# The up stage of a quantised FFN in reverse order, by half tiles, and the first parts of the down stage put ahead of a branch

## The chip, the core and the metric

The kernel runs on one NeuronCore of a Trainium2 chip. The metric is the device time of one execution in microseconds (us); the time given for a kernel is the median of its runs.

## What is computed

Two blocks with residuals on x of 2 x 2048 rows of 512. First cross-attention with layernorm, then the block that matters here:

```
x    = act_qdq(layernorm(x))                  # 16-bit: one scale for the whole tensor
up   = act_qdq(x @ lpbq_dequant(w_up).T)      # w: 4-bit, 1536 x 512
gate = act_qdq(x @ lpbq_dequant(w_gate).T)
sig  = fixed_qdq_u16(sigmoid(gate))
p    = act_qdq(gate * sig)
o    = act_qdq(p * up)
y    = x_in + o @ lpbq_dequant(w_down).T
def act_qdq(x): s = max(max(abs(x)) / 32767, 1e-12); return clip(round(x / s)) * s
```

Every `act_qdq` needs the maximum over its whole tensor before one element of it can be rounded. So nothing of p can be rounded before all of gate is there, and nothing of o before all of p and all of up are there.

## The kernel before

The 4096 rows are tokens. They are cut into NG = 8 groups of TG = 512 tokens for gate and up, and into 16 steps of TD = 256 tokens (two tiles of 128) for down. The 1536 features are NF = 12 chunks of 128, taken four at a time (NQ = 4), so there are NK = 3 tiles per group and 24 tiles `n = (t, k)` in all. Four stages follow each other:

1. **Front** (attention, layernorm, the transposed rows `hT`), up to about 176 us.
2. **Gate** (lines 507 to 552). The rounded input of a group is split into exact parts (`split_integers`, line 215: a high part, a low part and a combination), 3 MB per group, which go to the matmuls and are also written out (`parts_d`, line 536). `project` (line 496) makes 8 matmuls into a PSUM tile `q` and 4 into `e` for each feature chunk, 12 in all. The results go to `gate_d` (line 551). In the idle time the weights of up and down are prepared (`steps`) and written to `wu_d` and `wd_d`.
3. **Up** (lines 554 to 628). For each group t = 0 to 7 the parts are read back (`load_group`, line 560), and for each tile the gate is read back (`load_gate`, line 565). ScalarE makes `gi`, `sig` and `sq` of it (`gelu_like`, line 579), VectorE makes the integers `pi` of p (line 610). The matmuls make u two chunks at a time; ScalarE takes q out of PSUM (line 617) and VectorE subtracts e (line 618). PSUM holds two such halves (`ps_m`, bufs=2). u and pi are written out whole, 1 MB and 0.5 MB per tile (lines 619 and 611). Each tile gives the column n of `umax` (the maximum of u, line 620) and of `pumax` (a bound of the product, `max(abs(u) * pi)`, lines 621 to 623).
4. **Down** (lines 631 to 777). The scale of o needs the maximum of the rounded product. The kernel takes, in each partition, the tile with the largest bound: `best`, `where` and `row` (lines 653 to 658) name it, two indirect DMAs of GpSimd fetch it (lines 662 and 669), it is rounded and multiplied (lines 677 to 682), and the maximum over partitions is made by GpSimd (line 686). If the second largest bound cannot exceed that maximum, and two conditions on p hold, `flag` is 1 (line 698). All engines read the flag (line 701) and branch (line 702): with 0 a long general path is run, with 1 it is jumped over. Behind the branch the scales of o are made (lines 736 to 745). Then, for each of 16 steps, the next step's p, u and x are read (`load_step`, line 641: 3 + 3 + 1 DMAs), u is rounded (`ui`, line 752), and each of two tiles of 128 tokens gives `oi` (line 756), its parts (line 759), 24 matmuls into q, 12 into e (lines 764 and 768), and the output (lines 772 to 777).

The frame that records the kernel (tile pools, a scheduler) decides the order of instructions on each engine and puts in the waits; an engine runs its instructions in that order. Two things of the built order matter below. The DMAs of SyncE (the queue SP) use eight semaphores in turn, and each waits until the one before it on its semaphore has landed: at most eight are in flight. And where the general path is jumped over, each engine first waits until all that it issued ahead of the branch is done, and then adds to its semaphores what the general path would have added, so that later waits hold for both ways. A wait of another engine for work behind the branch thus waits for that engine to have passed the branch.

Of the kernel before, what the change touches and what calls it, by code (L numbers as in the profile page):

```python
# [61 lines left out]
P = 128  # L63
# [12 lines left out]
def tile_xattn_ffn(  # L76
# [41 lines left out]
    up_d = dram.tile([NG * NK, P, NQ, TG], F32, name="up_d")  # L118
    p_d = dram.tile([NG * NK, P, NQ, TG], I16, name="p_d")
# [8 lines left out]
    umax = const.tile([P, NG * NK], F32, name="umax")  # L128
    gtop = const.tile([P, NG * NF], F32, name="gtop")
    pumax = const.tile([P, NG * NK], F32, name="pumax")  # L130
# [99 lines left out]

    with ExitStack() as c0:
# [252 lines left out]
        wp_late = ctx.enter_context(tc.tile_pool(name="wp_late", bufs=NF - NE))  # L484
        hi_pool = c0.enter_context(tc.tile_pool(name="hi", bufs=1))
# [21 lines left out]
        with ExitStack() as c2:  # L507
# [6 lines left out]
            homes = [c2.enter_context(tc.tile_pool(name="parts0", bufs=1))]  # L514
# [9 lines left out]
            homes.append(c2.enter_context(tc.tile_pool(name="parts1", bufs=1)))  # L524
# [5 lines left out]
            steps = chain(split_rows(wpp, ps_t, w_up, wu_d, "u"), split_down(wpp, ps_t))  # L530
            for t in range(NG):
# [4 lines left out]
                nc.sync.dma_start(out=parts_d[t], in_=parts.bitcast(F32))  # L536
                for k in range(NK):
# [13 lines left out]
                    nc.sync.dma_start(out=gate_d[n], in_=g4)  # L551
            advance(steps, 1000)

    with ExitStack() as c3:
        pp = c3.enter_context(tc.tile_pool(name="parts", bufs=2))
# [4 lines left out]
        def load_group(t):  # L560
            parts = pp.tile([P, 3, ND, TG], F32R, tag="parts", name=f"parts_u{t}")
            nc.sync.dma_start(out=parts.bitcast(F32), in_=parts_d[t])
            return parts

        def load_gate(n):
            gt = wk2.tile([P, NQ, TG], F32, tag="gt", name=f"gt_{n}")
            nc.sync.dma_start(out=gt, in_=gate_d[n])
            return gt

        groups = {0: load_group(0)}  # L570
        wu = [load_parts(wu_d, f, "wu") for f in range(NF)]
        gts = {0: load_gate(0)}
# [25 lines left out]
        wd = []  # L598
        for t in range(NG):
            parts = groups.pop(t)  # L600
            if t + 1 < NG:
                groups[t + 1] = load_group(t + 1)
            for k in range(NK):
                n = t * NK + k
                if n + 1 < NG * NK:
                    gts[n + 1] = load_gate(n + 1)
                u4 = wk2.tile([P, NQ, TG], F32, tag="u4", name=f"u4_{n}")
                gi, sq = gelu_like(wk2, wk1, gts.pop(n), [NQ, TG], n)
                pi = wk2.tile([P, NQ, TG], I16, tag="pi", name=f"pi_{n}")
                nc.vector.scalar_tensor_tensor(pi, gi, k_p, sq, ALU.mult, ALU.mult)  # L610
                nc.sync.dma_start(out=p_d[n], in_=pi)
                for i in range(0, NQ, 2):
                    q = ps_m.tile([P, 2, TG], F32, tag="q", name=f"q_u{n}_{i}")
                    e = ps_m.tile([P, 2, TG], F32, tag="e", name=f"e_u{n}_{i}")
                    for j in range(2):
                        project(wu[NQ * k + i + j], parts, q[:, j, :], e[:, j, :])
                    nc.scalar.activation(u4[:, i : i + 2, :], q, AF.Copy, scale=1.0 + 1.0 / BASE)  # L617
                    nc.vector.tensor_tensor(u4[:, i : i + 2, :], u4[:, i : i + 2, :], e, ALU.subtract)  # L618
                nc.sync.dma_start(out=up_d[n], in_=u4)
                abs_max(umax[:, n : n + 1], u4, AX.XY)  # L620
                ua = wk2.tile([P, NQ, TG], F32, tag="ua", name=f"ua_{n}")
                nc.scalar.activation(ua, u4, AF.Abs)
                nc.vector.tensor_tensor_reduce(ua, ua, pi, 1.0, 0.0, ALU.mult, ALU.max, pumax[:, n : n + 1])
                if t == NG - 1:
                    for f in range(NQ * k, NQ * (k + 1)):
                        w = chunk_tile([P, 3, D], "wd", f)
                        nc.sync.dma_start(out=w.bitcast(F32), in_=wd_d[f])
                        wd.append(w)


    with ExitStack() as c5:
        wk1 = c5.enter_context(tc.tile_pool(name="wkd1", bufs=1))
        wk2 = c5.enter_context(tc.tile_pool(name="wkd2", bufs=2))
        ps_y = c5.enter_context(tc.tile_pool(name="ps_y", bufs=4, space=PSUM))

        def load_p(t, v):
            g, i = divmod(t * TD, TG)
            for k in range(NK):
                nc.sync.dma_start(out=v[:, ts(k, NQ), :], in_=p_d[g * NK + k, :, :, ds(i, TD)])  # L639

        def load_step(t):
            g, i = divmod(t * TD, TG)
            pi = wk2.tile([P, NF, TD], I16, tag="p5", name=f"p5_{t}")
            load_p(t, pi)
            uv = wk2.tile([P, NF, TD], F32, tag="u5", name=f"u5_{t}")
            for k in range(NK):
                nc.sync.dma_start(out=uv[:, ts(k, NQ), :], in_=up_d[g * NK + k, :, :, ds(i, TD)])  # L647
            x1 = wk2.tile([P, TD // P, D], F32, tag="x1", name=f"x1_{t}")
            nc.sync.dma_start(out=x1, in_=x1_d[g, :, ds(i // P, TD // P), :])
            return pi, uv, x1  # L650


        best = const.tile([P, 8], F32, name="best")
        nc.vector.max(best, pumax)
        where = const.tile([P, 8], U32, name="where")
        nc.vector.max_index(where, best, pumax)
        row = const.tile([P, 1], U32, name="row")
        nc.vector.scalar_tensor_tensor(row, where[:, 0:1], float(P), lane, ALU.mult, ALU.add)
        a_u, = over_partitions(umax, name="u")
        with tc.tile_pool(name="best", bufs=1) as bp:  # L660
            ub = bp.tile([P, NQ * TG], F32, name="ub")
            nc.gpsimd.indirect_dma_start(
                out=ub,
                out_offset=None,
                in_=up_d.rearrange("n p i t -> (n p) (i t)"),
                in_offset=bass.IndirectOffsetOnAxis(ap=row, axis=0),
            )
            pb = bp.tile([P, NQ * TG], I16, name="pb")
            nc.gpsimd.indirect_dma_start(
                out=pb,  # L670
                out_offset=None,
                in_=p_d.rearrange("n p i t -> (n p) (i t)"),
                in_offset=bass.IndirectOffsetOnAxis(ap=row, axis=0),
            )
            s_u, r_u = act_scale(a_u, "u", unit)
            ui = bp.tile([P, NQ * TG], I16, name="ui_b")
            nc.scalar.activation(ui, ub, AF.Copy, scale=r_u)

            nc.vector.tensor_tensor(ub, pb, ui, ALU.mult)

            two = const.tile([P, 2], F32, name="two")
            nc.vector.tensor_reduce(two[:, 0:1], ub, AX.X, ALU.max, apply_absolute_value=True)
            nc.vector.tensor_scalar(two[:, 1:2], best[:, 1:2], r_u, 1.0 + 2.0**-18, ALU.mult, ALU.mult)
            nc.vector.tensor_scalar(two[:, 1:2], two[:, 1:2], 0.5 * (QMAX + 2.0), None, ALU.add)
        top = const.tile([P, 2], F32, name="top")
        nc.gpsimd.partition_all_reduce(top, two, P, bass_isa.ReduceOp.max)
        a_o = const.tile([P, 1], F32, name="a_o")
        nc.vector.tensor_copy(a_o, top[:, 0:1])

        neg = const.tile([P, 1], F32, name="neg")  # L690
        nc.vector.tensor_scalar(neg, r_p, NEG_P, 1.0, ALU.mult, ALU.add)
        nc.vector.tensor_scalar(neg, neg, QMAX, top[:, 1:2], ALU.mult, ALU.max)
        sure = const.tile([P, 1], F32, name="sure")
        nc.vector.tensor_tensor(sure, neg, a_o, ALU.is_le)
        ok_p = const.tile([P, 1], F32, name="ok_p")
        nc.vector.tensor_scalar(ok_p, p_top, MIN_P, None, ALU.is_ge)
        flag = const.tile([P, 1], I32, name="flag")
        nc.vector.tensor_tensor(flag, sure, ok_p, ALU.mult)

        loaded = {0: load_step(0)}  # L700
        known = nc.values_load(flag[0:1, 0:1], min_val=0, max_val=1)  # L701
        with tc.If(known == 0):
            with tc.tile_pool(name="gen", bufs=1) as gp:
                pmax = gp.tile([P, NG * NF], F32, name="pmax")
                omax = gp.tile([P, NG * NF], F32, name="omax")

                def load(m, src, name):
                    v = gp.tile([P, TG], F32, tag="v", name=f"v{name}_{m}")
                    nc.sync.dma_start(out=v, in_=src[m // NQ, :, m % NQ, :])
                    return v  # L710
# [90 lines left out]
```

## Time and profile before

| | |
|---|---|
| median of 3 runs | 1046.68 us (1046.64 to 1049.0) |
| the profiled execution | 1046.88 us, of which the span is 1045.1 us, at a mean granted TensorE clock of 0.956 |
| TensorE (PE) busy | 944.2 us, 90% of the span |
| VectorE (DVE) / ScalarE (ACT) / GpSimd (POOL) busy | 796.2 / 541.9 / 75.2 us |
| DMA | 281.83 MB, 270 GB/s over the span |
| chain that ended last | 25% PE, all of it in the down stage |

How to read it: times count from the span's start. A row of the timeline has start, duration, engine, line, operation, output<-inputs, count, and in brackets how long the engine was idle before it and what ended that. "PEld" is the weight load, "SPq" the queue of DMAs that SyncE issues; an engine name with a q is its sequencer. Slices of view 2 are 26 us each.

### The profile page before, as it was taken

How to read it: one execution, taken by the hardware profiler on the slowest of the kernel's cores; microseconds unless marked ns; L12 is line 12 of the kernel's file. 1: busy time of each engine (PE TensorE's matmuls, PEld its weight loads, DVE VectorE, ACT ScalarE, POOL GpSimd, SP SyncE). 2: the span in 40 equal slices, each digit the busy share in tenths (PEclk: the TensorE clock that was granted, in tenths of full speed). 3: DMA queues.
4: the chain of work that ended last, by engine and by line, in shares of the span. 5: the costliest groups of instructions: out<-in, count | busy, mean ns of one | idle time of the engine just before them, and what ended most of it. 6: DMA issues, size and time to landing. Idle time of an engine off the chain costs nothing. (4 is left out here: it accounts for less than half of the span.)

```text
span 1045.1 us, 11428 instructions
## 1 busy us (share of the span) xinstructions
PE 944.2 (90%) x4320; PEld 764.4 (73%) x4320; DVE 796.2 (76%) x909; ACT 541.9 (52%) x582; POOL 75.2 (7%) x66
## 2 busy tenths in 40 slices
PE   6997975999999999996999999998029999999998
PEld 6765643888888878875878888887028888888886
DVE  4588857899989988445877789779269778887782
ACT  2278786333323332236798888987234444344431
POOL 0101110000000000000000000000001221112211
PEclk9999986999999999998999999999559999999999
DMA  9196546877985887897988898889989676766520
GB/s 332 31 350 254 212 172 257 330 278 296 357 322 201 317 315 299 316 389 285 387 298 336 315 379 321 322 317 358 354 261 293 202 230 193 231 195 198 173 80 31
DMA packets 118110, 281.83 MB, mean 270 GB/s; under 512 B 5408, under 2 KB 72992, under 8 KB 105632
## 3 DMA queue, kind: packets, MB, share of 16 engines
q1 hardware_dynamic: 117232, 278.42, 73.0%
q0 software_dynamic: 288, 1.57, 0.4%
q10 hardware_dynamic: 528, 1.05, 0.3%
q8 instruction: 34, 0.56, 0.2%
q14 instruction: 28, 0.23, 0.1%
HBM read 147.85 MB, written 133.17 MB: 269 GB/s over the span
## 5 line engine op out<-in xcount | busy, mean ns | idle before, releaser
L764 PE MATMUL yq<-wd,parts_o 128*128 128x512 f32 x768 | 182.0, 393 | 48.6 <-DMA u<-up_d 48.6
L764 PEld LDWEIGHTS yq<-wd,parts_o 128*128 128x128 f32 x768 | 145.8, 190 | 79.8 <-ACT parts_o L222 49.0
L501 PE MATMUL q_u<-parts_u,wu 128*128 128x512 f32 x768 | 192.4, 393 | 9.8 <-ACT u L617 8.5
L501 PE MATMUL q_g<-parts_g,wg 128*128 128x512 f32 x768 | 194.3, 394 | 5.2 <-ACT parts_g L222 5.2
L501 PEld LDWEIGHTS q_u<-parts_u,wu 128*128 128x128 f32 x768 | 144.7, 189 | 42.7 <-ACT u L617 11.4
L501 PEld LDWEIGHTS q_g<-parts_g,wg 128*128 128x128 f32 x768 | 144.6, 189 | 36.3 <-issue 5.6
L545 ACT ACTIVATE g<-q_g 128x512 f32<-128x512 f32 x96 | 57.3, 599 | 180.3 <-PE q_g L501 175.9
L505 PE MATMUL e_g<-parts_g,wg 128*128 128x512 f32 x384 | 105.2, 393 | 0.0
L505 PE MATMUL e_u<-parts_u,wu 128*128 128x512 f32 x384 | 103.1, 390 | 0.3 <-DVE u L618 0.3
L546 DVE CUSTOM_DVE_ANT_0 g<-g,e_g 128x512 f32<-128x512 f32 x96 | 64.5, 679 | 37.3 <-PE e_g L505 36.7
L768 PE MATMUL ye<-wd,parts_o 128*128 128x512 f32 x384 | 92.2, 389 | 0.0
L610 DVE SCALAR_TENSOR_TENSOR pi<-gi,k_p,sq 128x2048 int16<-128x2048 int16 x24 | 56.3, 2347 | 45.8 <-ACT sq L586 45.8
L505 PEld LDWEIGHTS e_u<-parts_u,wu 128*128 128x128 f32 x384 | 72.4, 189 | 15.8 <-DVE u L618 0.7
L768 PEld LDWEIGHTS ye<-wd,parts_o 128*128 128x128 f32 x384 | 72.1, 188 | 15.0
L505 PEld LDWEIGHTS e_g<-parts_g,wg 128*128 128x128 f32 x384 | 72.2, 189 | 14.8
L772 ACT ACTIVATE yqs<-yq,q_o 128x512 f32<-128x512 f32 x32 | 22.1, 689 | 117.1 <-PE yq L764 117.1
L618 DVE TENSOR_TENSOR u<-u,e_u 128x1024 f32<-128x1024 f32 x48 | 58.4, 1217 | 13.7 <-ACT u L617 13.5
L774 POOL TENSOR_TENSOR qx<-yqs,x 128x512 f32<-128x512 f32 x32 | 50.1, 1567 | 226.0 <-ACT yqs L772 226.0
L222 ACT CAST parts_o<-sa_o 128x1536 fp32r<-128x1536 int16 x32 | 47.1, 1474 | 35.8 <-PE ye L768 31.6
L776 DVE SCALAR_TENSOR_TENSOR y<-ye,e_o,qx 128x512 f32<-128x512 f32 x32 | 24.0, 751 | 54.0 <-PE ye L768 44.4
L617 ACT ACTIVATE u<-q_u 128x1024 f32<-128x1024 f32 x48 | 48.1, 1017 | 30.9 <-PE q_u L501 27.9
L756 DVE SCALAR_TENSOR_TENSOR oi<-p,k_o,ui 128x1536 int16<-128x1536 int16 x32 | 58.0, 1819 | 4.5 <-ACT ui L752 2.6
(165 smaller groups left out, 1280.0 us busy)
## 6 DMA issues: line engine op xcount, KB each, us to landing
parts_d<-parts_g SPq DMA_DIRECT2D x8, 3072.0 KB, 11.1
gate_d<-g SPq DMA_DIRECT2D x24, 1024.0 KB, 5.1
parts_u<-parts_d SPq DMA_DIRECT2D x8, 3072.0 KB, 13.5
gt<-gate_d SPq DMA_DIRECT2D x24, 1024.0 KB, 10.6
up_d<-u SPq DMA_DIRECT2D x24, 1024.0 KB, 7.0
u<-up_d SPq DMA_DIRECT2D x48, 512.0 KB, 6.8
p_d<-pi SPq DMA_DIRECT2D x24, 512.0 KB, 4.3
p<-p_d SPq DMA_DIRECT2D x48, 256.0 KB, 3.8
```

What stands on the lines that cost most here:

```text
L222: nc.scalar.copy(parts[:, 0, c], a[:, c])
L501: nc.tensor.matmul(q, lhsT=w[:, s, c, :], rhs=parts[:, s, c, :], start=(c + s == 0), stop=(c + s == ND))
L505: nc.tensor.matmul(e, lhsT=w[:, 2, c, :], rhs=parts[:, 2, c, :], start=(c == 0), stop=(c == ND - 1))
L545: nc.scalar.activation(g4[:, i, :], q, AF.Copy, scale=1.0 + 1.0 / BASE)
L546: nc.vector.tensor_tensor_reduce(g4[:, i, :], g4[:, i, :], e, 1.0, LOWEST, ALU.subtract, ALU.max, gtop[:, m : m + 1])
L610: nc.vector.scalar_tensor_tensor(pi, gi, k_p, sq, ALU.mult, ALU.mult)
L617: nc.scalar.activation(u4[:, i : i + 2, :], q, AF.Copy, scale=1.0 + 1.0 / BASE)
L618: nc.vector.tensor_tensor(u4[:, i : i + 2, :], u4[:, i : i + 2, :], e, ALU.subtract)
L756: nc.vector.scalar_tensor_tensor(oi, pi[:, :, ts(j, P)], k_o, ui[:, :, ts(j, P)], ALU.mult, ALU.mult)
L764: nc.tensor.matmul(q, lhsT=parts[:, s, f, :], rhs=wd[f][:, s, :], start=(f + s == 0), stop=(f + s == NF))
L768: nc.tensor.matmul(e, lhsT=parts[:, 2, f, :], rhs=wd[f][:, 2, :], start=(f == 0), stop=(f == NF - 1))
L774: nc.gpsimd.tensor_tensor(qx, qs, x1[:, j, :], ALU.add)
```

## The change

- **Order.** The up stage runs over the groups from 7 down to 0. The parts of groups 6 and 7 stay in SBUF, in two homes of 24 KB per partition each, and are not written to `parts_d`; the weights of up are loaded inside the last gate group. The tiles of p and up are numbered by `j`, in the new order, and the down stage takes the groups in it too. The first two gate tiles are read on GpSimd's queue.
- **Half tiles.** `up_d`, `p_d` and the columns of `pumax` are by halves of a tile (two chunks): 48 of each. u is written by halves; p is still written by one DMA per tile; the step's reads become 6 + 6 + 1 DMAs. ScalarE's absolute value and VectorE's bound are made per half (`bound`).
- **Gelu ahead.** `next_gelu` makes gi, sig and sq one tile ahead of its use.
- **Last half.** The last half of u (c = 47) has no column in `pumax`; it stays in SBUF as `u_last`, and its products are made there exactly. `best` is taken over the other 47 halves as soon as the 47th bound is there, and the fetch is half as large.
- **Maximum of u.** GpSimd's reduction over partitions is replaced by a transpose on TensorE (`rows_u`) and a reduction by VectorE.
- **Branch.** The reads of the first down step are issued in the last group of up (t = 0); the scales of o and the parts of the first tile (in three pieces) stand ahead of the branch.

```diff
-                nc.sync.dma_start(out=parts_d[t], in_=parts.bitcast(F32))
+                if t < NG - 2:
+                    nc.sync.dma_start(out=parts_d[t], in_=parts.bitcast(F32))
+                else:
+                    groups[t] = parts
...
+                    if t == NG - 1:
+                        wu += [load_parts(wu_d, f, "wu") for f in range(NQ * k, NQ * (k + 1))]
...
+        gts = [load_gate(*at, nc.gpsimd) for at in order[:2]]
...
+        def bound(c, u, pi):
+            ua = wk2.tile([P, 2, TG], F32, tag="ua", name=f"ua_{c}")
+            nc.scalar.activation(ua, u, AF.Abs)
+            nc.vector.tensor_tensor_reduce(ua, ua, pi, 1.0, 0.0, ALU.mult, ALU.max, pumax[:, c : c + 1])
+            return ua
...
+        for j, (t, k) in enumerate(order):
+            if k == 0:
+                parts = groups.pop(t)
+                if t + 1 < NG and t > 0:
+                    groups[t - 1] = load_group(t - 1)
+                if t == 0:
+                    home1.__exit__(None, None, None)
+                    lds.append(ctx.enter_context(tc.tile_pool(name="ld0", bufs=1, side="right")))
+                    load_step(0)
+            u4 = wk2.tile([P, NQ, TG], F32, tag="u4", name=f"u4_{j}")
+            if j:
+                pi = integers_of_p(j)
+            for h in range(2):
+                c = 2 * j + h
+                both = slice(2 * h, 2 * h + 2)
...
+                if c + 1 < NH:
+                    nc.scalar.activation(u4[:, both, :], q, AF.Copy, scale=1.0 + 1.0 / BASE)
+                    nc.vector.tensor_tensor(u4[:, both, :], u4[:, both, :], e, ALU.subtract)
+                else:
+                    for i in range(2):
+                        v = u_last[:, i, :]
+                        nc.scalar.activation(v, q[:, i, :], AF.Copy, scale=1.0 + 1.0 / BASE)
+                        nc.vector.tensor_tensor(v, v, e[:, i, :], ALU.subtract)
+                        abs_max(umax[:, LAST + 1 + i : LAST + 2 + i], v)
+                nc.sync.dma_start(out=up_d[c], in_=u4[:, both, :] if c + 1 < NH else u_last)
+                if h == 0:
+                    next_gelu()
...
+                elif c + 2 == NH:
+                    with tc.high_priority():
+
+                        u_last = bound(c, u4[:, both, :], pi[:, both, :])
+                        ub, pb = fetch_best()
...
+        rows = ps_m.tile([P, 2, TG], F32, tag="q", name="rows_u")[:, 0, :P]
+        nc.tensor.transpose(rows, m_u.to_broadcast([P, P]), ident)
...
+        for i, (uv, pv) in enumerate([last, (ub, pb)]):
+            ui = wk2.tile([P, NQ, TG], I16, tag="gi", name=f"ui_b{i}").rearrange("p i t -> p (i t)")[:, : 2 * TG]
+            nc.scalar.activation(ui, uv, AF.Abs, scale=r_u)
+            nc.vector.tensor_tensor_reduce(uv, ui, pv, 1.0, 0.0, ALU.mult, ALU.max, two[:, i : i + 1])
...
+        def round_o(tiles, pi, ui, pieces=1):
+
+            oi, a, parts = tiles
+            cs = [ts(i, NF // pieces) for i in range(pieces)]
+            for c in cs:
+                nc.vector.scalar_tensor_tensor(oi[:, c], pi[:, c], k_o, ui[:, c], ALU.mult, ALU.mult)
+                nc.vector.tensor_scalar(a[:, c], oi[:, c], 1.0 / BASE, None, ALU.mult)
+                nc.scalar.copy(parts[:, 0, c], a[:, c])
+                nc.vector.scalar_tensor_tensor(parts[:, 1, c], a[:, c], -BASE, oi[:, c], ALU.mult, ALU.add)
+            for c in cs:
+                nc.vector.scalar_tensor_tensor(parts[:, 2, c], a[:, c], BASE + 1.0, oi[:, c], ALU.mult, ALU.subtract)
+            return parts
...
+        ui_first = up_tile(0)
+        round_up(ui_first[:, :, :P], loaded[0][1][:, :, :P])
...
+        scales_of_o(a_o)
+
+        first = o_tiles(0)
+        round_o(first, loaded[0][0][:, :, :P], ui_first[:, :, :P], 3)
+
         known = nc.values_load(flag[0:1, 0:1], min_val=0, max_val=1)
```

## The prediction

> **What bounds the kernel now.** I read the page first (PE busy 90%), then the table by stages, because an average of 90% says nothing about where the other 10% are. Columns are busy us of PE, weight load, DVE, ACT and POOL, then granted clock, DMA share and GB/s. The rows are the start of the up stage, its rest, the passage to down, and down:
>
> ```profile
> 452.78:494.68 41.90, 32.94 (x145) 26.95 (x145) 21.29 (x27) 22.72 (x18) 0.37 (x1) 0.93 0.85 330
> 494.68:728.32 233.64, 232.57 (x1008) 190.12 (x1008) 194.36 (x129) 199.61 (x127) 0.00 (x0) 0.99 0.89 337
> 728.32:776.92 48.60, 0.00 (x1) 0.00 (x0) 21.40 (x34) 14.25 (x9) 2.96 (x4) 0.53 0.85 305
> 776.92:1041.00 264.08, 264.00 (x1152) 217.84 (x1152) 203.94 (x155) 107.94 (x78) 50.15 (x32) 0.99 0.60 188
> ```
>
> In the second and fourth stretch PE is busy nearly throughout: matmuls set the time. In the third it does nothing for 48.6 us. The waits of PE between 450 and 780 us name the idle places:
>
> ```profile
> PE yq L764 <- DMA u<-up_d: 48.6, 1, 48.6
> PE q_u L501 <- ACT u L617: 8.5, 2, 8.1
> PE q_u L501 <- DVE gtop L546: 0.9, 1, 0.9
> ```
>
> The releaser named for the 48.6 us is only the event that came last by the profile; what the time consists of is seen in the timeline:
>
> ```profile
> 729.77 1.91 ACT L622 ACTIVATE ua<-u 128x2048 f32<-128x2048 f32 x1 [1.29 <-DVE u L618]
> 731.58 1.99 ACT L582 ACTIVATE gi<-gt,r_g 128x2048 int16<-128x2048 f32 x1
> ...
> 737.58 2.35 DVE L610 SCALAR_TENSOR_TENSOR pi<-gi,k_p,sq 128x2048 int16<-128x2048 int16 x1 [3.96 <-ACT sq L586]
> ...
> 742.81 0.16 DVE L658 SCALAR_TENSOR_TENSOR row<-where,lane 128x1 uint32<-128x1 uint32 x1
> ...
> 747.45 1.29 POOL L662 DMA_INDIRECT ub<-up_d,row  x1 [14.72 <-issue]
> 749.04 0.94 POOL L669 DMA_INDIRECT pb<-p_d,row  x1 [0.30 <-issue]
> ...
> 757.05 2.00 ACT L677 ACTIVATE ui_b<-ub,r_u 128x2048 int16<-128x2048 f32 x1 [19.50 <-DMA ub<-up_d,row]
> ...
> 764.69 0.16 DVE L698 TENSOR_TENSOR flag<-sure,ok_p 128x1 int32<-128x1 f32 x1
> 768.37 2.85 ACT L752 ACTIVATE ui<-u,r_u 128x3072 int16<-128x3072 f32 x1 [9.32 <-ACTq L702]
> ```
>
> From the last matmul of up (E = 728.32) the passage falls into four legs: to the row's number 14.65 (end 742.97; the gelu of the last tile is still to be made), to the fetch 4.48 (u and p must have landed), the fetch 9.60, rounding and reducing to the flag 7.80 (end 764.85), and from the flag to the first matmul 12.07. The sum is 48.6. The last leg holds the branch, which the rows of line 702 show:
>
> ```profile
> L702 DVEq COMPARE_BRANCH x1: 72/72/72, 765.5 to 765.5; - x1
> L702 DVEq EVENT_SEMAPHORE x1: 21/21/21, 768.7 to 768.7; - x1
> ```
>
> Between a sequencer's compare and its next instruction 2.7 (ACT) to 3.2 us (DVE) pass; from the flag DVE works again after 3.91 us, ACT after 3.52.
>
> **Up stage.** Ideal is 1152 matmuls at 2.72 us per 12 (the chain's rows), 261.1 us; from 452.78 to 728.32 it took 275.5. The 14.4 lost are the 0.9 and 8.1 above, 2.1 for a slow clock after the 8.1 (8 matmuls 3.78 instead of 1.98, 4 in 1.39 instead of 1.07), and 3.3 in small pieces. The 8.1 come from order: the first gate tile arrives only for 479.01, behind the weights and 3 MB of parts on SP, so p is late, and u's write waits behind p's on SP, so the third u finds no buffer.
>
> With the change, parts, weights and two gate tiles are on chip at the end of gate. GpSimd's reduction a_g stands behind its two gate reads, but these wait only for tiles 21 and 22 of gate, made 22 and 11 us before its end; I cost that at nothing (cover gone: 1 to 2 us). I walk the built order with the rows' durations, from the end of gate: r_g is there at 4.8 as before, ACT's first eviction at 7.0 to 8.0 (459.80 in the trace), then two gi, a sigmoid, an absolute value and sq (2.0 + 2.0 + 2.0 + 1.0 + 1.9 = 8.9), then the second eviction, done at 17.9. PE wants that PSUM half at 0.9 + 3 x 5.44 = 17.2: 0.7 late. VectorE then makes pi (2.35) ahead of the subtractions, and the next e tiles come 0.4, 0.7 and 0.6 late before it catches up. Sum 2.4. Later nothing should wait: per tile of 10.88 us of PE, ACT has 2 x 1.02 + 2.0 + 2.0 + 1.9 + 2 x 1.02 = 10.0 (before 9.85), DVE 2 x 1.22 + 2.35 + 2.29 + 2 x 1.2 = 9.5 (before 9.4). Slack is thin, so I charge 1.1 more. New length 0.9 + 261.1 + 3.5 = 265.5: **10.0 us gained**, bounds 4 and 12. The omitted 2 x 3 MB of parts writes and reads gain nothing by themselves: DMA ran at 337 GB/s here without ending a wait of PE, and what remains (89 MB in 265 us, 335 GB/s) asks for no more.
>
> **The passage, leg by leg, from the new E.** (1) p is ready early, so the row waits for half 46: PE is done with it at -5.44, but in the built order DVE still has pi, a bound and a maximum in front; the walk gives the subtraction at -0.8, the half maximum 1.2, the bound 1.2, and 0.7 for best and row as in the trace: row at +3.6 (0 to 4.5). (2) Half 46 must land. It leaves at +0.5, behind four weight loads of wd (3.1 MB, from about -6) and p. At the 0.41 MB/us of the busy slices here that is drained at about +4; 1.2 us of GpSimd's start as before (u landed about 746.2, issue 747.45): fetch at +6.7 (3 to 8). (3) The fetch took 9.6 for 1 MB beside full DMA engines; half a MB less at about half their rate is 2.5 less: u at +13.7, p, issued 1.6 later, at +15.3 (11 to 18). (4) Rounding is beside p's landing; bound 1.2, reduction over partitions and its hand-over 0.5, then 0.5: flag at +17.5. u_last, the transpose and the scale are done by about +12 under the fetch; without that cover they would cost up to 4. No row shows such a transpose; the 128-row matmul cannot be below zero, and 1 us above stays under cover.
>
> (5) Here the change promises most and, I think, gives nothing. The parts now stand ahead of the branch, but on DVE and ACT that means ahead of their own reading of the flag. In the built order PE's second matmul waits for a count of DVE that only the skipped-path instruction behind DVE's branch reaches. So from the flag: scales 0.9; three pieces, each 0.75 for oi, 0.25, 0.68 and 0.68 (thirds of 1.82, 0.56, 1.75 and 1.75 with some fixed cost), 7.0; then the flag and branch, 3.9. That is 11.8 against 12.07. First matmuls at +29.3. **48.6 - 29.3 = 19.3 us gained**, bounds 15 and 27.
>
> **Down.** PE has 32 x 8.16 = 261.1 us and was never short. The second tile's oi waits for DVE's branch and for SP's, which now lets five reads of u land first: about flag + 12 both, parts at flag + 16, wanted at flag + 23. The second step's p is issued behind that, parts at flag + 27, wanted at flag + 31. No loss (bounds 0 and 3). The clock: in the Trainium skill, "TensorE: Matmul & The Clock Gate", Part 1, a cold array runs at half rate until about 3.4 us of sustained work, 1.7 us lost. The rows here: the first 24 matmuls take 8.32 instead of 5.44, 2.9 lost. A gap of 29 us is still cold, so either price is paid before and after, and I count no gain.
>
> Against half tiles speaks "DMA: Bandwidth & Descriptors", section Bandwidth: batch to 1 MiB, fixed 2 us per transfer. By its fit (2 us + bytes/436 GB/s) a down step now has 15 DMAs worth 38 us in a row, more than its 16.3. But before it was 9 worth 26, also more, and PE did not wait: transfers overlap. The nearest row, 512 KB of u landing in 6.8 us, with eight in flight gives 15 x 6.8 / 8 = 12.8 us per step, under 16.3. I take the row: nothing.
>
> **Sum.** Against the profiled execution: 1046.88 - 10.0 - 19.3 = 1017.6; it lies 0.2 above the median, so **1017.4 us**.
>
> **Rivals.**
> (A) Chance 0.60: as worked out, 1009 to 1026 with its bounds.
> (B) 0.14: parts ahead of the branch do hide. PE's start would then be flag + 4.5, 7.3 less: 1010. The work order speaks for it, the wait on DVE's count against.
> (C) 0.18: ACT, at 10.0 of 10.88, never pays back its start and is in DVE's way at the end; the up stage keeps the old loss and u's half lands late: 10 less gained, 1027.
> (D) 0.06, slower: DMA count in down. Each step's 15 DMAs at eight in flight take longer than PE when one needs over 16.3 x 8 / 15 = 8.7 us. The largest before was 8.2, of twice the size. To eat 29 us over 16 steps it must be 9.7; at 10.5 us a step lasts 19.7, 16 x 3.4 = 54 lost: 1072. Half sizes and a DMA share of 0.60 speak against it.
> (E) 0.02: the sum of such mishaps leaves about 1046; that the long general path is taken would show as far above all of these.
>
> 0.3% (3.1 us) is what a measurement of this kernel can tell from no change. Faster 0.92, within 0.02, slower 0.06. The range, 1008 to 1028, holds A, most of B, and C.
>
> **What would show it.** Right: up stage of about 265 us with waits of PE under 1 us each; the fetch at E + 7; the flag at E + 17; and between flag and first matmuls still 11 to 12 us, with DVE's compare at the end of its parts. B is right if that is under 6. C if PE waits for ACT all through up. D if SP waits for DMAs in down and PE has gaps. Wrong altogether if u's last halves land over 10 us after E.

## The result, and the profile after

| | before | after |
|---|---|---|
| median of the runs compared (us) | 1047.56 (4 runs, 1046.64 to 1049.0) | 1033.94 (4 runs, 1030.94 to 1036.44) |
| ratio, 95% interval | | 0.9868 (0.9838 to 0.9897) |
| the profiled execution, its span | 1046.88, 1045.1 | 1033.99, 1032.2 |
| gate: length | 277.1 | 280.1 |
| up, from the end of gate to the last matmul | 275.5 | 269.2 |
| passage, no matmul of a stage | 48.6 | 35.2 |
| down, to its last matmul | 263.8 | 266.0 |

The change makes the kernel 1.3% faster. I had forecast 1017.4 with a range from 1008 to 1028: the direction is right, the size is not, and the time lies outside the range. Here are the stages of the kernel after, as the table by stages gives them (us, then busy us of PE, weight load, DVE, ACT and POOL, granted clock, DMA share, GB/s). The first row is gate, which I had not listed for before because I expected nothing of it:

```profile
177.33:457.40 280.07, 280.01 (x1248) 227.71 (x1248) 234.63 (x312) 88.13 (x132) 1.40 (x2) 0.99 0.77 287
457.40:726.59 269.19, 265.99 (x1153) 216.35 (x1152) 220.32 (x204) 227.24 (x170) 0.37 (x1) 1.00 0.87 327
726.59:761.78 35.19, 0.61 (x2) 0.18 (x2) 16.79 (x44) 9.12 (x10) 3.45 (x3) 0.54 0.75 296
761.78:1027.81 266.03, 264.26 (x1152) 217.72 (x1152) 205.14 (x155) 107.86 (x78) 52.94 (x32) 0.99 0.60 189
```

The end of up, E, is put here at 726.59, and in the variants at the same place. The record of the last matmul ends 0.16 us later, at 726.75, and that end is what the 275.5 and 48.6 of before and the forecast count from. By it up is 269.4 and the passage 35.0; no reading below hangs on the difference.

PE is busy throughout gate and almost throughout up, and both are still longer than 1152 matmuls at before's rate: that is a loss no list of waits can show. The waits that there are, of PE between 440 and 1030 us (total, times, longest):

```profile
PE yq L877 <- ACTq L821: 28.8, 1, 28.8
...
PE q_u L507 <- ACT u L708: 2.3, 1, 2.3
PE yq L877 <- ACT parts_o L788: 1.3, 1, 1.3
PE q_u L507 <- DVE gtop L556: 0.9, 1, 0.9
PE yq L877 <- DVE parts_o L789: 0.5, 1, 0.5
```

The 8.1 of before is a 2.3 now, as the walk of the built order had it (2.4). The long wait is still the passage, in the timeline:

```profile
726.94 0.32 SPq L716 DMA_DIRECT2D up_d<-u  x1
...
729.54 0.16 DVE L673 SCALAR_TENSOR_TENSOR row<-where,lane 128x1 uint32<-128x1 uint32 x1
...
740.51 2.10 POOL L678 DMA_INDIRECT best<-up_d,row  x1 [279.22 <-DMA wd<-wd_d]
...
749.43 1.15 ACT L752 ACTIVATE ui_b<-best,r_u 128x1024 int16<-128x1024 f32 x1 [11.15 <-DMA best<-up_d,row]
...
752.55 0.22 DVE L814 SCALAR_TENSOR_TENSOR flag<-top,floor,a_o 128x1 int32<-128x1 f32 x1
...
761.78 2.50 PE L877 MATMUL yq<-wd,parts_o 128*128 128x512 f32 x5 [28.83 <-ACTq L821]
```

From the last matmul of up (E = 726.59) the row is ready at +3.1, but GpSimd starts the fetch only at +13.9; u lands at +22.8, the flag is done at +26.2, PE starts at +35.2. Half 46 is the first row shown: it left at +0.4, and the list of DMAs gives its time from issue to landing:

```profile
up_d<-u SPq DMA_DIRECT2D x1, 512.0 KB, 12.5
```

So it landed at about +12.8, and GpSimd's start took another 1.1. (The profile names a weight load of wd as the releaser. But GpSimd waits for several semaphores here, which writes and loads use in turn, and the last weight load issued ahead of half 46, at 723.5, took 13.0 and so had landed by 736.5.)

The second loss is in the rate. A stretch of PE in gate of the kernel before, where all groups run alike, and two stretches of up in the kernel after, first one of group 5, whose parts lie in the second home, then one of group 4, in the first:

```profile
301.46 1.98 PE L501 MATMUL q_g<-parts_g,wg 128*128 128x512 f32 x8
303.27 1.07 PE L505 MATMUL e_g<-parts_g,wg 128*128 128x512 f32 x4
304.18 1.98 PE L501 MATMUL q_g<-parts_g,wg 128*128 128x512 f32 x8
...
541.46 2.04 PE L507 MATMUL q_u<-parts_u,wu 128*128 128x512 f32 x8
543.33 1.10 PE L511 MATMUL e_u<-parts_u,wu 128*128 128x512 f32 x4
544.27 2.03 PE L507 MATMUL q_u<-parts_u,wu 128*128 128x512 f32 x8
...
574.76 1.98 PE L507 MATMUL q_u<-parts_u,wu 128*128 128x512 f32 x8
576.58 1.07 PE L511 MATMUL e_u<-parts_u,wu 128*128 128x512 f32 x4
577.48 1.98 PE L507 MATMUL q_u<-parts_u,wu 128*128 128x512 f32 x8
```

From one group of eight to the next it is 2.72 us before (304.18 - 301.46), 2.81 (544.27 - 541.46) in the second home of after and 2.72 (577.48 - 574.76) in its first, without a wait in between and, in both stretches of after, at a granted clock of 1.00. All odd groups of gate and up are like the one in the second home, all even ones like the other; before, all were 2.72. An odd group is 12 x 12 matmuls and takes 33.73 us, an even one 32.67: eight passes of odd groups, four in each stage, cost some 8.5 us.

The difference to the forecast, 16.4 us of the profiled execution, is then complete: 1.6 of a later start of gate (gate starts anywhere from 175.5 to 178.4 in the runs below, and from 175.7 to 177.4 with before and its shifted variants, so no cause was sought), 3.0 in gate, 3.7 in up, 5.9 in the passage and 2.2 in down.

### The profile page after: what moved, and what is told of

Same layout as the page of the kernel before. It is cut to its first block, busy times and chain, and to the rows that moved or that the text cites. A ratio compares the mean times of both kernels' runs of the same rounds, so it can differ in the third digit from the quotient of the medians.

```text
span 1032.2 us, 11748 instructions
## 1 busy us (share of the span) xinstructions
PE 950.3 (92%) x4321; PEld 764.7 (74%) x4321; DVE 798.0 (77%) x968; ACT 541.8 (52%) x610; POOL 79.9 (8%) x67
## 5 line engine op out<-in xcount | busy, mean ns | idle before, releaser
L507 PE MATMUL q_g<-parts_g,wg 128*128 128x512 f32 x768 | 197.0, 397 | 5.0 <-ACT parts_g L225 5.0
L507 PE MATMUL q_u<-parts_u,wu 128*128 128x512 f32 x576 | 144.5, 393 | 0.0
L507 PEld LDWEIGHTS q_u<-parts_u,wu 128*128 128x128 f32 x576 | 108.3, 188 | 24.5
L511 PE MATMUL e_u<-parts_u,wu 128*128 128x512 f32 x288 | 78.1, 393 | 0.0
L662 DVE CUSTOM_DVE_ANT_0 ua<-ua,pi 128x1024 f32<-128x1024 f32 x47 | 56.9, 1221 | 18.8 <-ACT ua L661 18.8
L788 ACT CAST parts_o<-sa_o 128x1536 fp32r<-128x1536 int16 (+1 forms) x34 | 47.4, 1398 | 45.1 <-PE ye L881 27.6
L887 POOL TENSOR_TENSOR qx<-yqs,x 128x512 f32<-128x512 f32 x32 | 52.9, 1654 | 222.1 <-ACT yqs L885 222.1
L786 DVE SCALAR_TENSOR_TENSOR oi<-p,k_o,ui 128x1536 int16<-128x1536 int16 (+1 forms) x34 | 59.5, 1754 | 10.0 <-ACT ui L772 4.3
L511 PEld LDWEIGHTS e_u<-parts_u,wu 128*128 128x128 f32 x288 | 54.1, 188 | 12.2
```

The lines of the kernel that those rows point to most:

```text
L507: nc.tensor.matmul(q, lhsT=w[:, s, c, :], rhs=parts[:, s, c, :], start=(c + s == 0), stop=(c + s == ND))
L511: nc.tensor.matmul(e, lhsT=w[:, 2, c, :], rhs=parts[:, 2, c, :], start=(c == 0), stop=(c == ND - 1))
L786: nc.vector.scalar_tensor_tensor(oi[:, c], pi[:, c], k_o, ui[:, c], ALU.mult, ALU.mult)
L788: nc.scalar.copy(parts[:, 0, c], a[:, c])
L887: nc.gpsimd.tensor_tensor(qx, qs, x1[:, j, :], ALU.add)
```

## The experiments

Two theories. **Q**: the fetch is late because half 46 waits behind queued transfers, and the eight weight loads of wd in the last tiles are what fills the queue; its rival is that the row, GpSimd or the fetch itself is slow. **H**: the odd groups are slow because of where the second home lies, its address or its place; its rivals are that anything else of the new order (the transfers beside it, the kept parts) slows them. Two smaller questions are whether the parts ahead of the branch hide anything, and whether SyncE's reads ahead of it do harm. Single executions of one kernel lie up to 5.5 us apart (after: 1030.94 to 1036.44), so where a run was made once its stages are compared, not its time.

### The address of the home

In the built programs the second home of after begins at byte 204768 of each partition, 32 beyond a multiple of 64; the first at 92992, a multiple of 64. **The kernel after with the second home moved down by 32 bytes:**

```diff
+            pad1 = tc.tile_pool(name="pad1", bufs=1, side="right")
+            nc.gpsimd.memset(pad1.__enter__().tile([P, 8], F32, name="pad1"), 0.0)
             home1 = tc.tile_pool(name="parts1", bufs=1, side="right")
```

> The changed kernel with a pad of 32 bytes per partition ahead of the second home of the parts, which so begins at a multiple of 64 bytes (204736 instead of 204768). Theory: with the home 32 bytes off, 12 matmuls of an odd group take 2.81 us instead of 2.72, one part in 32 more, so that 8 odd group passes (4 in gate, 4 in up) cost 12 x 0.09 = 1.1 us each; expected 8.6 us less than the changed kernel (about 1025.3), all blocks at 2.72. Rival: it is the place at the far end of SBUF, or traffic beside it, not the 32 bytes: no difference (1033.9), odd groups still at 2.81.

Measured: ratio 0.9854 (0.9831 to 0.9877) to before; odd groups 2.79 to 2.80 per 12 matmuls, even ones 2.72. A multiple of 64 alone takes away only an eighth to a quarter of the loss.

**The kernel before, its two gate homes moved up by 32 bytes** (the same pad ahead of `parts0`):

> The kernel before with 32 bytes put ahead of its two homes of the gate stage, so that both begin 32 bytes off a multiple of 64; the up stage's buffers stay where they were. Theory of the 32 bytes: all 96 blocks of 12 matmuls in gate go from 2.72 to 2.81 us, gate longer by 8.6 us and no other stage (1047.6 to about 1056). Rival (place or traffic): no difference.

Measured: ratio 1.0064 (1.0047 to 1.0081), gate 283.0 instead of 277.1, all its groups 2.80, up untouched at 2.72:

```profile
300.52 2.03 PE L501 MATMUL q_g<-parts_g,wg 128*128 128x512 f32 x8
302.38 1.09 PE L505 MATMUL e_g<-parts_g,wg 128*128 128x512 f32 x4
303.32 2.03 PE L501 MATMUL q_g<-parts_g,wg 128*128 128x512 f32 x8
```

Only addresses (and a pad that is written once) were changed, in a kernel with the old order: 32 bytes can cost 3% of the rate of the matmuls and 2% of the stage, and the new order as a cause is not needed. In this kernel the tiles stacked above the homes (gate results, weights in preparation) moved by 32 bytes with them; in the variants of after below, the built programs differ from after in the second home and the pad alone.

**Other pads**, of 96, 1312 and 4128 bytes in the kernel after, and of 64 in the kernel before:

> The kernel after the change with the second home of the parts moved down by 96 bytes, to byte 204672 of each partition (a multiple of 128, 0x780 within 2 KB); nothing else changes. Every matmul of gate and up reads 2 KB of these parts per partition, so its start within 2 KB is that of the home. In after the odd groups, which read this home, take 2.811 us per 12 matmuls, the even ones 2.72. Theory L (the low bits of the address decide, and 128 is the unit): a multiple of 128 is at least as good as 64 beyond one, odd groups at 2.72, gate 4 us and up 4 us shorter, time 1026. Theory M (the place near the top of the memory decides): odd groups stay at 2.79 to 2.81, time 1033 to 1034. Theory N (the distance to the next 2 KB boundary decides): also slow, 2.79, and told from M by the next run.

> The same with the second home moved down by 1312 bytes, to 203456, whose low eleven bits (0x2C0) are those of the homes of the kernel before, where every group took 2.72 us per 12 matmuls. The place in the memory is nearly that of after. Theory L or N (low bits, of whatever kind): odd groups fall to 2.72, gate to 276 and up to 265, time 1026. Theory M (the place): odd groups stay at 2.79 to 2.81 and the time at 1033 to 1034.

> The kernel before the change with its two gate homes moved up by 64 bytes (to 129792 and 154368, multiples of 128, 0x300 within 2 KB); the move by 32 bytes slowed all gate groups from 2.72 to 2.80 us per 12 matmuls. Theory: a start that is a multiple of 64 is fast at this place, so 2.72 and a time of 1047. Rival: 64 beyond a multiple of 128 is what is wanted (as in all fast homes so far: 0x2C0 and 0x340), so 2.80 and 1054.

> The kernel after the change with the second home moved down by 4128 bytes, to 200640, which is 64 beyond a multiple of 128 like all homes of the kernel before (2.72 us per 12 matmuls at 92864 to 154304), and like 204736 and 203456 (2.79 to 2.80). If the place in the upper part of the memory decides, odd groups stay at 2.79 to 2.80 and the time at 1031 to 1033. If only what lies within the last 4 KB does, 2.72 and 1025.

Measured (one run each), with the two kernels above, in us per 12 matmuls; the second column is what is left of the address when it is divided by 128:

| home at byte | within 128 | us per 12 |
|---|---|---|
| 92864, 117440 (up, before), 92992, 129728, 154304 | 64 | 2.72 |
| 129792, 154368 (before, +64) | 0 | 2.75; the first group 2.80 |
| 204672 (after, 96 down) | 0 | 2.75 |
| 129760, 154336 (before, +32) | 32 | 2.80 |
| 200640, 203456, 204736 (after, 4128, 1312 and 32 down) | 64 | 2.79 to 2.80 |
| 204768 (after) | 96 | 2.81 |

With the pad of 96, a stretch of group 3 reads so:

```profile
600.92 1.99 PE L507 MATMUL q_u<-parts_u,wu 128*128 128x512 f32 x8
602.75 1.08 PE L511 MATMUL e_u<-parts_u,wu 128*128 128x512 f32 x4
603.67 1.99 PE L507 MATMUL q_u<-parts_u,wu 128*128 128x512 f32 x8
```

That is 2.75, and this run's gate is 277.8 and its up 265.6, 2.2 and 3.6 less than after: up is as long as I had forecast, with 1.3 of the slow rate left and a shorter wait (1.6). Its time was 1030.06. Only the home was moved here, so it is shown that its place changes the rate of the odd groups. Theory L of the expectation fell in its strict form (128 is better than 32 or 96, but not as good as before), and the run at 203456, with the low eleven bits of before's homes, fell too: 2.80. A theory of the place alone fails as well, since 204672 and 204736 lie 64 bytes apart. What holds in all six rows: starts that are 32 beyond a multiple of 64 are slow everywhere, and 64 beyond a multiple of 128 is the best start below byte 155000 and a bad one above byte 200000. Multiples of 128 give 2.75 in both halves of the memory, but not always. In the kernel before with 64 bytes, group 0 of gate ran at 2.80 and group 2 at 2.75, with both in the home at 129792:

```profile
201.25 2.03 PE L501 MATMUL q_g<-parts_g,wg 128*128 128x512 f32 x8
203.12 1.10 PE L505 MATMUL e_g<-parts_g,wg 128*128 128x512 f32 x4
204.05 2.03 PE L501 MATMUL q_g<-parts_g,wg 128*128 128x512 f32 x8
...
260.66 1.99 PE L501 MATMUL q_g<-parts_g,wg 128*128 128x512 f32 x8
262.49 1.08 PE L505 MATMUL e_g<-parts_g,wg 128*128 128x512 f32 x4
263.41 1.99 PE L501 MATMUL q_g<-parts_g,wg 128*128 128x512 f32 x8
```

So the address matters, but it does not fix the rate by itself. What else does, and why a start 64 beyond a multiple of 128 differs by place, stays open.

### The queue ahead of the fetch

**The eight loads left out**, to see the passage without them:

```diff
                 for f in range(NQ * k, NQ * (k + 1)):
+                    if k:
+                        wd.append(wd[f % NQ])
+                        continue
                     w = chunk_tile([P, 3, D], "wd", f)
```

> Leaves out the loads of the down weights 4 to 11; the down matmuls use chunks 0 to 3 three times, as many as before. It measures the passage with no weight traffic. Theory (queued bytes): half 46 lands within 4 us of its issue, fetch at about E + 5, and it takes 4 to 5 us instead of 8.9, so the flag stands at E + 13 instead of E + 26, first down matmul at E + 22 instead of E + 35. Rival (slow writes, slow indirect fetch): fetch not before E + 12, and 8 to 9 us long.

Measured: 1018.69 (one run), with half 46 landing 5.5 us after its issue, and this timeline (E = 723.71):

```profile
730.22 1.07 POOL L678 DMA_INDIRECT best<-up_d,row  x1 [269.74 <-DVE m_u L744]
...
735.31 1.13 ACT L755 ACTIVATE ui_b<-best,r_u 128x1024 int16<-128x1024 f32 x1
...
738.41 0.22 DVE L817 SCALAR_TENSOR_TENSOR flag<-top,floor,a_o 128x1 int32<-128x1 f32 x1
...
748.71 3.78 PE L880 MATMUL yq<-wd,parts_o 128*128 128x512 f32 x8 [18.63 <-ACTq L824]
```

The fetch starts at +6.5 (forecast: 6.7), ScalarE takes its u up 5.1 later instead of 8.9 (it landed after 4.3, when ScalarE was still busy), the flag is at +14.9, PE starts at +25.0; down takes 263.8. Passage and down together are 288.8 us instead of 301.2. So the row, GpSimd and the engines' legs are as forecast or better, and 12.4 us of the kernel after are the price of 6.3 MB that must pass just here. Theory Q holds, its rival falls.

**The loads behind the last half of u**, all eight:

```diff
-            if t == 0:
-                for f in range(NQ * k, NQ * (k + 1)):
+            if t == 0 and k != 1:
+                for f in range(NQ) if k == 0 else range(NQ, NF):
```

> The changed kernel with the loads of the down weights 4 to 7 moved behind the last write of u, to those of 8 to 11. Theory: the write of half 46 lands 12.5 us after its issue because 3 MB of weights and what stands before them are drained first; without them it lands by 6 us, GpSimd's fetch starts at about E + 7 instead of E + 13.9, and the first down matmul comes 5 to 7 us earlier (about 1028), unless the fetch, then beside 6 MB of weights, gets longer by the same. Rival: writes of u are slow by themselves: fetch still at E + 12 or later, time 1034.

Measured: ratio 0.9814 (0.9798 to 0.9831), median 1028.04. The passage (E = 724.39), half 46 landing in 5.1 us:

```profile
730.47 1.07 POOL L678 DMA_INDIRECT best<-up_d,row  x1 [270.32 <-DVE m_u L741]
...
739.42 1.15 ACT L752 ACTIVATE ui_b<-best,r_u 128x1024 int16<-128x1024 f32 x1 [3.35 <-DMA best<-up_d,row]
...
743.20 0.22 DVE L814 SCALAR_TENSOR_TENSOR flag<-top,floor,a_o 128x1 int32<-128x1 f32 x1
...
751.75 4.56 PE L877 MATMUL yq<-wd,parts_o 128*128 128x512 f32 x9 [21.01 <-ACTq L821]
```

The fetch starts at +6.1, so the 7.8 us of the loss that came ahead of it are gone. Of the rest, 2.4 in the passage and 5.8 in down against the run without the loads stay: u needs 9.0 us instead of 5.1, because the loads now run beside the fetch, and in down PE waits once 3.3 us for parts: in the built order of this kernel all reads of the second step come behind the branch, its p lands late, and VectorE's `oi` waits 3.9 us for it. Passage plus down 296.9.

**The loads behind the fetch, or behind the maximum.** Two tries to get the rest. In the first the loads stand on GpSimd's queue after the two fetches; in the second they are held until GpSimd's reduction, by a write of one element that they overwrite. Both with a moved home (203456 and 204672).

```diff
+            nc.gpsimd.tensor_copy(w[:, 0, 0:1], top[:, 0:1])
+            nc.gpsimd.dma_start(out=w.bitcast(F32), in_=wd_d[f])
```

> The kernel after the change with its eight last weight loads of down (6.3 MB) put on GpSimd's queue behind the two fetches, and the second home at 203456 as in the run before. Theory (what delayed the fetch was the drain of the loads queued ahead of half 46, and where all eight were put behind the last half they met the fetch itself): the fetch starts 6.5 us after the last matmul of up as without these loads, takes 8 us, the flag is at +15.5, first matmul at +25.5. The loads then need 6.3 MB at 0.41 MB/us, 15 us from +9, all there at +25 to +27, before PE wants the fifth chunk at +28: no wait in down. Gap 25.5 instead of 35.2: 9.7 less than after by the passage, 1024; and 8 less, 1016, if the home's address is the cause of the slow odd groups. Rival (the loads still take the fetch's share of the DMA engines, or GpSimd's eight issues hold up its reduction of the maximum): fetch to flag 12 us or more, the gap 28 to 30, PE waits for weights at down's start: 1020 to 1028.

> The kernel after the change with its eight last weight loads of down on GpSimd's queue, held there until its reduction of the two maxima is done (one element of each weight buffer is written from the result first, and the load overwrites it), and the second home of the parts at 204672 (a multiple of 128). Theory (the drain of queued loads delays the fetch, and nothing else on the path needs them early): fetch starts 6.5 us after the last matmul of up, reduction at +14, flag at +15, first matmul at +25, as without the loads. The loads are issued from +15 to +21; 6.3 MB at 0.41 MB/us are there at +31, the fifth chunk at about +19. Down as after, 264 to 266. Against after's 1033.9: passage 10 less, the slow groups 5.5 less: 1018, 1015 to 1021. Rival (PE or the other engines wait for these loads behind the branch, or the first steps' reads of p and u queue behind them): PE waits 5 us or more in down, 1023 to 1026.

Measured: 1034.34, ratio 0.9857 (0.9841 to 0.9874), and 1034.16, ratio 0.9873 (0.9857 to 0.9890). Both missed. In the first of them the built order put GpSimd's loads ahead of its fetch after all (705.8 to 724.8, one whenever a buffer of the up weights came free); with two queues feeding the DMA engines, half 46 was behind still more:

```profile
up_d<-u SPq DMA_DIRECT2D x1, 512.0 KB, 19.4
```

The fetch started at E + 21.4, PE at +41.6. It is not the test that was meant, but it is one more point on Q: more loads ahead of half 46, a later fetch. In the second the passage came out nearly as expected (fetch +6.8, flag +15.0, PE +26.2), and the cost appeared in down, 278.2 us:

```profile
PE yq L885 <- DMA wd<-wd_d: 5.0, 4, 1.6
PE yq L885 <- ACT parts_o L796: 3.9, 1, 3.9
```

PE starts and finds the last weights missing, chunk after chunk, with the granted clock at 0.71 in its first 16 us (after: 0.84). In both, as in the run without the loads, the built order also put twelve reads of u (the second and third step, 3.1 MB) ahead of the branch, where after has five; they compete with the loads, and the second step's p comes behind them. The run without the loads shows that these reads do no harm by themselves; what share of the 12 us in down is theirs and what the loads' these runs do not separate.

### The branch and its parts

**The parts of the first tile behind the branch** (`round_o` of the first tile moved into the loop, whole):

> The changed kernel with the first tile's parts made behind the branch again, as a whole and not in pieces; the scales stay ahead of it. From the flag to the first down matmul the changed kernel takes 9.0 us, the kernel before 12.1. Theory of the prediction (the branch still stands behind the parts on DVE and ACT, so putting them ahead saves little): 3.5 us of branch, then 1.8 + 0.6 + 1.5, so 7.5 to 9.5, the same within 1 us. Rival (the parts were hidden behind the reading of the flag): 3 us or more longer, 12 us and over.

Measured: 1034.41 (one run), from the end of the flag to the first matmul 10.3 us instead of 9.0. But this built order differs in one more thing: VectorE makes `oi` of both tiles of the step before the parts of the first.

```profile
755.35 3.55 DVE L786 SCALAR_TENSOR_TENSOR oi<-p,k_o,ui 128x1536 int16<-128x1536 int16 x2 [3.99 <-DVEq L818]
```

In the kernel after, the second tile's `oi` (1.8 us) comes behind the first matmul. So the parts ahead of the branch hide 1.3 us at most, and this run does not show that they hide anything. The rows of the branch in the kernel after:

```profile
L821 DVEq COMPARE_BRANCH x1: 72/72/72, 758.6 to 758.6; - x1
...
L821 DVEq EVENT_SEMAPHORE x1: 21/21/21, 761.9 to 761.9; - x1
```

VectorE's last part ends at 759.75 (in the timeline). Its sequencer compares at 758.6, 1.1 us before that, and the 3.3 us of the branch run from there. So about a third of the branch lies under the parts, and most of it doesn't.

**The second step's reads of u behind the branch.** Five of them stand ahead of it, and SyncE waits for their landing before it passes. A buffer that is only free behind the branch holds them back:

```diff
+        u5_1 = lds[1].tile([P, NF, TD], F32, tag="u5", name="u5_1")
         ui_first = up_tile(0)
...
+                nc.vector.memset(u5_1, 0.0)
                 load_p(0, loaded[0][0])
```

> The changed kernel with the second step's reads of u held behind the branch, by a write to their tile on the path that is jumped over. Theory: SP waits for five reads of u ahead of its skipped path until 763.4, so the second step's p is issued 10.8 us after the flag and PE waits 1.8 us in the first tiles of down; with the reads behind, p is issued by about 5 us after the flag and the two waits of PE (0.5 and 1.3) are gone: 1 to 2 us less. Rival: u is then late instead, and the waits stay or grow.

Measured: 1038.64 (one run), passage 34.5, down 273.2, with one wait of PE of 7.9 us for parts: u of the second step is late. The early reads are worth keeping.

### Together

**Home 32 down, loads late, reads behind the branch:**

> The changed kernel with all three: aligned home, late weights 4 to 7, second step's u behind the branch. If the three act on different stretches: 1033.9 - 8.6 - 5 - 1.5, about 1019. If only the alignment acts, 1025.

Measured: ratio 0.9828 (0.9811 to 0.9844), 1028.57, no better than the loads alone. **Home 96 down and loads late:**

> The kernel after the change with the eight last weight loads of down behind the write of the last half of u on SP's queue, and the second home at 204672. The loads alone gave 1028.0, the home alone 1030.1 against 1033.9. If the two add, 1024.2, with gate at 277.8, up at 265.6, passage at 27.4 and down at 269.6. If the move of the home works only through something else that the loads change too, it stays at 1028.

Measured: ratio 0.9819 (0.9803 to 0.9836), 1028.29. The rate and the passage came as expected (gate 277.7, passage 27.7, down 269.2), but up took 268.6, not 265.6. Its first group is 5.0 us longer than the other odd ones (38.03 beside 32.98), 3.1 of them PE's wait for ACT and the rest the slow clock after it; with the loads late alone it was 1.7. That wait lies anywhere from 0 to 3.1 us in these runs, and what sets it I did not trace. Neither can be told apart from the kernel after with only the loads moved, which stays the simplest of the three: some 1028, 0.5% under the kernel after (the intervals of 0.9814 and 0.9868 do not meet).

## Why the prediction was wrong

**Up stage: right in mechanism, 3.7 us too short.** Forecast 265.5 = 0.9 + 261.1 + 3.5. Measured 269.2: 0.9, 261.1, 4.3 for the four odd groups at 33.73 instead of 32.67, 2.3 for the wait (2.4 forecast) and 0.6 of small pieces (1.1 charged). What failed is the term 1152 x 2.72 / 12: I took a matmul to cost the same wherever its data lie. Moving the home alone brought these groups to 32.98 us and the up stage, with a shorter wait, to 265.6. The same cost appears in gate, which I left out of the sum altogether because the change moves no work there: it was +3.0.

**Passage:** 13.4 gained (48.6 to 35.2), less than the lower bound of 15. **Leg 1: right.** Row at +3.1, forecast +3.6.

**Leg 2: the step that failed.** "It leaves at +0.5, behind four weight loads of wd ... At the 0.41 MB/us of the busy slices here that is drained at about +4 ... fetch at +6.7". The rate was right: the DMA engines moved 0.42 MB/us in this stretch. The amount was not. At landing in 12.5 us, 12.5 x 0.42 = 5.2 MB stood ahead of half 46's end, not the 2 MB of a landing at +5.5 (5.0 x 0.41): two halves of u, four loads, p and the half itself. I counted the four loads as if the queue were empty when they came at -6. But the queue had been filling since the reads of the first down step at 699, and three of the first four loads, a write of p and two of u, 3.9 MB, still stood in it: the first of the four loads that I counted took 10.6 us to land. DMA ran at 1.02 of its share from 715 on. The fetch came at +13.9, outside my bounds (3 to 8), and half 46 landed more than 10 us after E, the sign that the prediction gave for being wrong altogether. The row to read was there: in the trace of before, between 700 and 735 us, a load of wd took 9.0 us (median of 8) from issue to landing. At 0.42 MB/us the load itself is 1.9 of these, and most of the rest must be what stood ahead of it. (The writes of p took 2.9 in the same list, so the queue was not full all the time.) The run without the loads gave +6.5.

**Leg 3: 1.9 too short.** u landed 8.9 after the start, 7.0 forecast; p half a microsecond behind it. Without the loads it was 4.3, with ScalarE ready at 5.1: the forecast lies between.

**Leg 4: as forecast.** From u's landing to the flag it took 3.3, forecast 3.8.

**Leg 5: too pessimistic by 2.8.** 9.0 instead of 11.8: scales 0.7 (0.9), pieces 6.3 (7.0), branch 2.0 (3.9). The claim that the parts ahead of the branch give nothing was nearly right (1.3 at most), but its ground was wrong in one point: the sequencer doesn't wait for its engine's last instruction before it reads and compares.

**Down: 2.2 lost, forecast 0 with a bound of 3.** Waits of 1.8 for the first parts. That half tiles slow the down stage by their transfers is refuted: down ran at 0.60 of DMA as before, and without the loads it took 263.8 as before. Rival D had no part in it: no read of u in down took more than 6.9 us (before, the largest of the whole stage was 9.3; the 8.2 of the prediction is from a part of it). The price of the slow clock was paid again, as forecast: the first 24 matmuls took 8.11 us, 8.32 before, instead of 5.44; the 1.7 us that the prediction set beside it is an estimate, half of the page's 3.4. In the Trainium skill, "DMA: Bandwidth & Descriptors", the fixed 2 us and the fit that the prediction quotes stand in the section "Anatomy of one DMA — SWDGE (gpsimd) path", for DMAs issued by GpSimd; only the rule of 1 MiB is in Bandwidth, and the 38 us are an estimate by that fit.

Of the rivals, C (up keeps its old loss, 1027) is nearest in time and wrong in cause: the half of u did land late, but by the queue, while PE waited for ScalarE once, 2.3 us. Of B's 7.3, the parts hid 1.3 at most. The bounds of A's terms add up to 1008 to 1031, more than the 1009 to 1026 given for it; the result lies outside these too.

The sum of the failed terms: 7.2 later fetch, 1.9 longer in its landing less 0.5 in what follows, -2.8 in leg 5 (unrounded, 5.9 for the passage); about 8 in rate, 3.0 and 3.7 of it in the stages' net lengths; 2.2 in down; 1.6 ahead of gate.

## What to carry to other kernels

Before you price a transfer on a path by the bytes put in front of it, read from the trace how long its neighbours take from issue to landing: if a 768 KB load takes 9 us where 0.42 MB/us pass, there are, by estimate, 2 to 3 MB ahead of it already, and what is issued next on that queue is late by what still stands there. Transfers that are needed late and issued early are not free: put them behind the one that the path waits for, but not so far that the first use meets them (here both extremes gave 1034, the middle 1028, though the late one also had more reads of u ahead of the branch). After an allocation changes, compare the time of a block of matmuls between the two traces: a loss of 3% in the rate shows in no wait.

## What was not expected of the hardware

- The rate of these 128x512 f32 matmuls depends on the byte at which the moving data begin: 2.72 us per 12 at the best starts, 2.75 at multiples of 128, 2.80 and 2.81 at 32 and 96 beyond one. A shift of both homes by 32 bytes cost the kernel before 0.64% (0.47 to 0.81). The best start below byte 155000 (64 beyond a multiple of 128) gave 2.80 above byte 200000, and one group gave 2.80 from a home that gave others 2.75; neither was explained.
- A write of 512 KB took 5.1 to 5.8 us to land, 12.5 or 19.4 as more loads were queued ahead of it; an indirect fetch of 512 KB 4.3 us with no loads and about 9 us among them (all by the list of DMAs).
- From an engine's compare to its next instruction it was 3.3 us on DVE, as in the kernel before (3.2), and the sequencer can compare while its engine still works.
